# A four-layer graph network on one Trainium2 core: transfers of 127 rows in two parts, a first stage with x on ScalarE's queue, and earlier score matrices

## The chip, the core and the metric

The kernel runs on one core of a Trainium2 chip. Such a core has TensorE (PE in the profile; its weight loads are shown apart as PEld), VectorE (DVE), ScalarE (ACT), GpSimd (POOL) and SyncE (SP). Each engine runs its own instructions strictly in order and waits on semaphores for the others. SP, ACT and POOL can also issue DMA transfers, which move data between DRAM and the on-chip memories. The metric is device time in microseconds for one execution.

## The reference

The input is a node matrix x of 3327 rows and 512 columns and an adjacency matrix of 3327 x 3327 integers. Four layers are applied, each as x = x + layer(relu(layernorm(x)), adj). Layers 0, 1 and 2 are graph attention with 8, 4 and 8 heads; layer 1 adds self loops to the adjacency. Layer 3 averages over the neighbours.

```python
# one attention layer (layer 0)
Wh = jnp.einsum('nd,hdo->hno', x, W)
f1 = jnp.einsum('hno,ho->hn', Wh, a1)
f2 = jnp.einsum('hno,ho->hn', Wh, a2)
e = leaky_relu(f1[:, :, None] + f2[:, None, :], 0.2)
e = jnp.where(adj[None] > 0, e, NEG_INF)
out = elu(einsum('hnm,hmo->hno', softmax(e, axis=-1), Wh))
# the last layer
agg = (adj > 0) @ x / maximum(deg, 1)
out = relu(concat([x @ W_self + b_self, agg @ W_nb + b_nb]) @ W_comb + b_comb)
```

## The kernel before, in words

**Tiles.** The 3327 nodes are 26 tiles of 128 rows; the last tile, number 25, has 127. Target nodes are taken in chunks of four tiles (`chunks`, the last of two); source tiles come in five groups of 6, 6, 6, 4 and 4 (`JG`).

**How attention is computed.** exp(leaky_relu(s1 + s2)) is a product of a factor of the target and a factor of the source, with one pair of factors where s1 + s2 is positive and another where it isn't. So for a chunk and a head the kernel makes two 0/2 matrices in fp8 for each group: the comparison of the score row s1 with each source's score (`gt`, ACT at L656, or DVE at L653 for the source tiles in `GP_ON_DVE`), then and-ed with the adjacency mask (`tht`, L662), then the rest of the mask (L666). PE multiplies these with the source's values, which are stored as three bf16 pieces (`ab`; L694 for `tht`, L697 for `gt`).

**First stage (from L818).** For each of 26 tiles of x: load it (`first_x`, L833, on SP's queue, up to six tiles ahead, seven buffers), layernorm statistics (`norm`: DVE L318 and L322, then three small POOL steps L323 to L325 on a tile called `mv`), relu (`normed`, ACT L330), transpose on PE (L137) and copy out (`hT`, ACT L141), project with the 512 weight columns and 8 + 8 score columns (`projected`, PE L388 into PSUM tiles `acc`), scale (`scaled`) and split into pieces (`pieces`; ACT L363 and L369, DVE L359, POOL L367), and store two tiles' pieces in DRAM (L375, 1600 KB, from SP). The score columns of the weights are made at the start by `fold` in `open_layer`: products on DVE and POOL (L299) and sums on DVE (L303). In the same stage `load_mask` makes 20 adjacency blocks: load on POOL's queue (`at`, L216), transpose on PE (L221), comparison on DVE (`st`, L225), store in DRAM (`mask`, L230); `mask_tiles` then loads them as `m` (L238). Four groups of pieces for head 0 are loaded ahead in this stage (`load_pieces`, L601).

**Layers 0 to 2 (`attention`).** Loops: chunk, head, pairs of tiles of the chunk, source tiles. Between pairs `hooks.run` emits steps of other work: adjacency blocks, and the next layer's stages for tiles whose chunk is done. `open_next` loads the next layer's weights at chunk 0, head 1, behind a mark called the gate. Each head needs one broadcast score row per chunk (`s1b`, L624, 256 KB).

**Last stage.** Masks times values on PE in fp32 (L921), two DVE operations per tile (L930, L931) and the store of 512 columns (L932, SP).

**Order.** The code gives the work; a scheduler places instructions on each engine by it, by data and by the marks that `after` sets. Waits on one engine hold back all that stands behind on it, DMA issues too.

Of the kernel before, what the change touches and what calls it, by code (L numbers as in the profile page):

```python
# [52 lines left out]
def tile_gnn(ctx: ExitStack, tc: tile.TileContext, x, adj, W0, a01, W1, al, ar, W2, a2,  # L53
# [48 lines left out]
    s1d = [dram.tile([NT, H, P], F32, name=f"s1_{l}") for l, H in enumerate(heads)]  # L102
# [45 lines left out]

    stored = {}
    gone = []  # L150
# [52 lines left out]
    def load_mask(pool, t, g):  # L203


        hooks.done += 1
        n = pn(t)
        c, k = where[t]
        j0, nj = JG[g]
        w = min(nj * P, N - j0 * P)  # L210
        at = pool.tile([P, JM * P], BF16, name="at", bufs=3)
        if n < P:
            nc.vector.memset(at, 0.0)
        elif w < nj * P:
            nc.vector.memset(at[:, w:nj * P], 0.0)
        ld = nc.gpsimd.dma_start(at[:n, :w], adj[t * P:t * P + n, j0 * P:j0 * P + w])  # L216
        if gone:
            after(ld, gone[-2] if len(gone) > 1 else stored[NT - 1])
        tp = ps.tile([P, 8, P], BF16, name="tp", bufs=2)
        for j in range(nj):  # L220
            tr = nc.tensor.transpose(tp[:, j, :], at[:, j * P:(j + 1) * P], identb)  # L221
            if j == 0 and gone:
                after(tr, gone[-1])
        st = pool.tile([P, JM, P], FP8, name="st", bufs=3)
        nc.vector.tensor_scalar(st[:, :nj], tp[:, :nj], 0.0, 2.0, op0=ALU.is_gt, op1=ALU.mult, saturate=False)  # L225
        if j0 <= t < j0 + nj:
            d = pool.tile([P, P], BF16, name="d", bufs=1)
            nc.vector.tensor_tensor(d, tp[:, t - j0, :], negI, ALU.is_gt)
            nc.vector.tensor_scalar(dg1[:, t, :], d, 2.0, None, op0=ALU.mult, saturate=False)
        nc.sync.dma_start(maskd[c][g][:, k], st[:, :nj])  # L230

    def mask_tiles(c, self_loops=False, early=False):
        t0, nt = chunks[c]
        tiles, loops = [], []
        for g, (j0, nj) in enumerate(JG):
            m = mk.tile([P, PER * JM * P], FP8, name="m")
            v = m[:, :nt * nj * P].rearrange("p (k j i) -> p k j i", k=nt, j=nj)
            ld = nc.sync.dma_start(v, maskd[c][g])  # L238
            if early and c == 0:
                after(ld, stored[21])  # L240
            if self_loops:
                for k in range(nt):
                    if j0 <= t0 + k < j0 + nj:
                        loops.append((v[:, k, t0 + k - j0, :].bitcast(U32), dg1[:, t0 + k, :].bitcast(U32)))
            tiles.append(v)
# [17 lines left out]
    def open_layer(l):  # L263
# [17 lines left out]
        for i in range(2):  # L281
            av.append(pre.tile([P, 2, H2, DK], F32, name="h"))
            ld = nc.sync.dma_start(av[i].rearrange("p f h d -> p (f h) d"), a_srcs[l][i].partition_broadcast(P))
            if l:
                after(ld, stored["gate"])
        for k in range(KC):
            for f in range(2):
                dst = L.w[:, k, f, :D // 2]
                if l == 0:
                    nc.sync.dma_start(dst.rearrange("p (g o) -> p g o", g=H2),  # L290
# [6 lines left out]
        def fold(i, k):  # L297
# [3 lines left out]
            if gone:  # L301
                after(m, gone[-1])
            nc.vector.tensor_reduce(L.w[:, k, :, D // 2 + i * H2:D // 2 + (i + 1) * H2], pr, AX.X, ALU.add)  # L303
        folds = [lambda i=i, k=k: fold(i, k) for i in range(2) for k in range(KC)]
        if l:
            hooks.small = folds
        else:
            for f in folds:
                f()
# [18 lines left out]
    def normed(xt, mv, pool, behind=None):  # L328
        h = pool.tile([P, D], F32, name="h", bufs=2)
        act = nc.scalar.activation(h, xt, AF.Relu, bias=mv[:, 3:4], scale=mv[:, 2:3])  # L330
        if behind:
            after(act, behind)
        return h
# [7 lines left out]
    def pieces(L, t, AB, pool, first, behind=None):  # L341
# [32 lines left out]
        elif first and o == two - 1:  # L374
            stored[t] = nc.sync.dma_start(abd[l][g][:, :, js, :].rearrange("h p j w -> p h j w"), pt).ins.name  # L375
# [3 lines left out]
    def projected(L, t, hT, first):  # L379
# [4 lines left out]
        pws = []  # L384
        for f in range(2):
            pw = (accs if first else ps).tile([P, D // 2 + H], F32, name="acc" if first else "mm")
            for k in range(KC):
                L.mm = nc.tensor.matmul(pw, hT[:, k, :], L.w[:, k, f, :], start=(k == 0), stop=(k == KC - 1)).ins.name  # L388
# [3 lines left out]
            pws.append(pw)  # L392
# [43 lines left out]
    def project_last(L, t, hT, i, behind=None):  # L436
# [10 lines left out]
        if i == 0:  # L447
            def add():
# [4 lines left out]
                nc.sync.dma_start(y1d[c][kk * P:kk * P + n, :], y[:n])  # L453
# [10 lines left out]
    def send_s1(L, t, pool, first):  # L464
# [10 lines left out]
        (nc.sync if first else nc.gpsimd).dma_start(s1d[L.l][t0:t0 + nt].rearrange("t h p -> (t h) p"), s1t[:nt * H])  # L475

    def node_stages(L, t, get_x, pool, first=False):
# [7 lines left out]
        def statistics():  # L485
            q["mv"] = norm(q["x"], pool, behind())
# [21 lines left out]
        if first:  # L508
            return [lambda: (q.update(x=get_x()), statistics(), relu()), turn,
                    lambda: parts(L, t, scaled(L, t, projected(L, t, q["hT"], first), pool, first), pool, first), send]  # L510
# [82 lines left out]
    ahead = {}  # L593

    def load_pieces(L, pool, g, h):
# [4 lines left out]
        v = tl[:, :nj * HW].rearrange("p (j w) -> p j w", j=nj)  # L600
        return v, nc.sync.dma_start(v, abd[L.l][g][h])  # L601

    def attention(L, hooks, open_next, close):
# [4 lines left out]
        masks = mask_tiles(0, l == 1, l == 0)  # L608
        for c, (t0, nt) in enumerate(chunks):
            W = nt * P  # L610
# [3 lines left out]
            for h in range(H):  # L614
# [8 lines left out]
                s1b = rp.tile([P, WMAX], F32, name="s1b", bufs=2)  # L623
                nc.sync.dma_start(s1b[:, :W].rearrange("p (k i) -> p k i", k=nt), s1d[l][t0:t0 + nt, h, :].partition_broadcast(P))  # L624
                ab = []
                for a in range(2 if l == 1 else 1):
                    row = []
                    for g, (_, nj) in enumerate(JG):
# [6 lines left out]
                        else:  # L635
                            v, ld = ahead.pop(g) if g in ahead else load_pieces(L, mp if l else bp, g, h)
                        row.append(v)
                    ab.append(row)
                if c == 0 and h == 1:
# [745 lines left out]
```

## Time and profile before

| | us |
|---|---|
| median of 3 runs (range) | 3609.15 (3607.2 to 3612.18) |
| the profiled execution, its own time | 3609.94 |
| its span, first to last instruction | 3608.1 |
| PE busy | 3470.2 |
| DVE busy | 2648.6 |
| ACT busy | 2511.8 |
| POOL busy | 603.0 |

The median is that of unprofiled runs; the profiled execution has a time of its own, and the span leaves out what lies around its instructions. Busy time is a union over the span. Instructions that only issue a DMA aren't counted as busy, though the engine's queue stands while they run. PE's granted clock was 0.988 of full speed on average.

### The profile page before, as it was taken

The numbers are of one execution on the slowest core, as the hardware profiler recorded it, in microseconds if no ns is written. First come the engines' busy times: TensorE is split into PE (matmuls) and PEld (weight loads), VectorE is DVE, ScalarE is ACT, GpSimd is POOL, SyncE is SP. The second block draws the span as 40 slices with busy tenths as digits, with TensorE's granted clock in tenths as the row PEclk, the third lists the DMA queues.
The fourth block names the chain that finished last, engine by engine and source line by source line (L and its number), as shares of the span: only waits on it lengthen the run. The fifth ranks groups of instructions, "written<-read, shape, count | busy, mean of one in ns | idle before, by whom it ended". The sixth has DMA issues, their size and how long they took to land. (4 is left out here: it accounts for less than half of the span.)

```text
span 3608.1 us, 78551 instructions
## 1 busy us (share of the span) xinstructions
PE 3470.2 (96%) x31291; PEld 3131.4 (87%) x31291; DVE 2648.6 (73%) x5227; ACT 2511.8 (70%) x4113; POOL 603.0 (17%) x855
## 2 busy tenths in 40 slices
PE   6799999999999999999999989999999999999998
PEld 5589999999999878888888869989898989876886
DVE  7688888888887779888888868867676768672211
ACT  5587787777787788888788767767676767572111
POOL 6511221111110111233222230001010101010000
PEclk9899999999999999999999999999999999999999
DMA  7687777878866877877777876655555555576331
GB/s 213 213 239 219 212 217 215 229 207 234 237 194 206 297 264 272 286 254 277 278 257 271 311 265 205 194 176 181 175 191 182 169 176 189 169 270 253 101 104 52
DMA packets 369431, 780.69 MB, mean 216 GB/s; under 512 B 35906, under 2 KB 207333, under 8 KB 368416
## 3 DMA queue, kind: packets, MB, share of 16 engines
q1 hardware_dynamic: 341024, 713.17, 59.4%
q0 software_dynamic: 28032, 62.41, 7.3%
q8 instruction: 249, 4.08, 0.4%
q14 instruction: 126, 1.03, 0.1%
HBM read 667.96 MB, written 129.64 MB: 221 GB/s over the span
## 5 line engine op out<-in xcount | busy, mean ns | idle before, releaser
L694 PE MATMUL acc<-ab,tht 128*128 128x195 bf16 (+1 forms) x10816 | 1840.4, 248 | 15.6 <-DVE tht L662 14.3
L697 PE MATMUL acc<-ab,gt 128*128 128x195 bf16 (+1 forms) x10816 | 1839.4, 248 | 6.6 <-DVE rc L734 4.3
L656 ACT ACTIVATE gt<-s1b,ks 128x512 fp8e4<-128x512 f32 (+1 forms) x2464 | 1457.4, 677 | 316.5 <-issue 158.6
L694 PEld LDWEIGHTS <-tht 128*128 128x128 fp8e4 x10816 | 1059.1, 98 | 28.9 <-DVE tht L662 15.9
L697 PEld LDWEIGHTS <-gt 128*128 128x128 fp8e4 x10816 | 1058.9, 98 | 26.5 <-issue 20.2
L662 DVE TENSOR_TENSOR tht<-gt,m 128x768 uint32<-128x768 uint32 (+3 forms) x560 | 447.4, 799 | 141.4 <-ACT gt L656 139.5
L666 DVE TENSOR_TENSOR gt<-tht,m 128x768 uint32<-128x768 uint32 (+3 forms) x560 | 448.9, 802 | 8.7
L590 ACT CAST ts<-tht 128x1536 fp32r<-128x1536 fp8e4 x208 | 300.3, 1471 | 55.9 <-PE acc L687 51.7
L687 PE MATMUL acc<-ab,ts 128*128 128x258 f32 x2496 | 334.2, 290 | 4.4 <-ACT ts L590 2.3
L653 DVE TENSOR_SCALAR gt<-s1b,ns 128x512 fp8e4<-128x512 f32 (+1 forms) x448 | 222.2, 501 | 149.6 <-PE acc L697 147.9
L687 PEld LDWEIGHTS acc<-ab,ts 128*128 128x128 f32 x2496 | 314.1, 191 | 13.4 <-ACT ts L590 3.0
L921 PE MATMUL acc<-y,mf 128*128 128x512 f32 x1352 | 309.8, 391 | 1.6 <-DVE mf L916 1.6
L656 ACT ACTIVATE tht<-s1b,ks 128x512 fp8e4<-128x512 f32 (+1 forms) x504 | 308.5, 681 | 2.8 <-DMA s1b<-s 2.3
L921 PEld LDWEIGHTS acc<-y,mf 128*128 128x128 f32 x1352 | 253.5, 188 | 57.8 <-DVE mf L916 2.0
L712 DVE TENSOR_REDUCE R<-acc 128x130 f32<-128x390 f32 x416 | 214.5, 555 | 91.6 <-PE acc L697 91.0
L797 POOL TENSOR_TENSOR xt<-xt,e 128x512 f32<-128x512 f32 x72 | 122.2, 1697 | 888.8 <-DVE e L796 567.5
L690 PE MATMUL acc<-ab,tht 128*128 128x387 bf16 x1248 | 226.1, 329 | 6.0 <-DVE tht L662 3.2
L918 ACT CAST mf<-m 128x768 fp32r<-128x768 fp8e4 (+1 forms) x78 | 59.1, 762 | 245.1 <-PE acc L921 233.3
L687 PE MATMUL acc<-ab,tv 128*128 128x258 f32 x1664 | 220.0, 283 | 3.3 <-DMA ab<-ab 2.2
L687 PEld LDWEIGHTS acc<-ab,tv 128*128 128x128 f32 x1664 | 207.5, 189 | 6.2 <-issue 2.1
L388 PE MATMUL mm<-w,hT 128*128 128x260 f32 (+1 forms) x832 | 198.4, 393 | 9.3 <-ACT hT L141 5.6
L690 PEld LDWEIGHTS <-tht 128*128 128x128 fp8e4 x1248 | 117.3, 98 | 83.3 <-DVE tht L662 3.6
(141 smaller groups left out, 3421.4 us busy)
## 6 DMA issues: line engine op xcount, KB each, us to landing
ab<-ab SPq DMA_DIRECT2D x336, 600.0 KB, 5.6
ab<-ab SPq DMA_DIRECT2D x224, 400.0 KB, 4.1
ab<-ab SPq DMA_DIRECT2D x112, 774.0 KB, 6.3
ab<-ab SPq DMA_DIRECT2D x112, 516.0 KB, 5.5
ab<-ab SPq DMA_DIRECT2D x56, 582.0 KB, 6.6
s1b<-s SPq DMA_DIRECT2D x120, 256.0 KB, 6.2
m<-mask SPq DMA_DIRECT2D x72, 384.0 KB, 4.2
ab<-pt SPq DMA_DIRECT2D x13, 1600.0 KB, 7.6
```

What stands on the lines that cost most here:

```text
L388: L.mm = nc.tensor.matmul(pw, hT[:, k, :], L.w[:, k, f, :], start=(k == 0), stop=(k == KC - 1)).ins.name
L590: (nc.scalar.copy if KIND[g] == "s" else nc.vector.tensor_copy)(t[:, :k1 - k0, :nj], th[a][g][:, k0:k1])
L653: nc.vector.tensor_scalar(gv[:, :, jj, :], s1v, L.ns2[:, j, h:h + 1], 2.0, op0=ALU.is_gt, op1=ALU.mult, saturate=False)
L656: nc.scalar.activation(gv[:, :, jj, :], s1v, AF.Relu, bias=L.ks2[:, j, h:h + 1], scale=BIG, saturate=False)
L662: nc.vector.tensor_tensor(pu, gu, mu, ALU.bitwise_and)
L666: nc.vector.tensor_tensor(gu, pu, mu, ALU.bitwise_xor)
L687: mm = nc.tensor.matmul(acc[k][:, :2 * DA], thr[g][:, k - ks[0], jj, :], ab[a][g][:, jj, :], start=(j == 0), stop=(j == NT - 1), skip_grou ...
L690: mm = nc.tensor.matmul(acc[k][:, :3 * DA], th[a][g][:, k, jj, :], ab[a][g][:, jj, :3 * DA], start=(j == 0), stop=(j == NT - 1), skip_grou ...
L694: nc.tensor.matmul(acc[k][:, :3 * DA + o], th[0][g][:, k, jj, :], ab[0][g][:, jj, :3 * DA + o], start=(j == 0), stop=False, skip_group_che ...
L697: mm = nc.tensor.matmul(acc[k][:, AO:AO + 3 * DA + o], th[1][g][:, k, jj, :], ab[0][g][:, jj, AO:AO + 3 * DA + o], start=False, stop=(j == ...
L712: nc.vector.tensor_reduce(R[:, k], v.rearrange("p a (s d) -> p a d s", s=3), AX.X, ALU.add)
L921: nc.tensor.matmul(acc[k], mf[:, jj, :], y2[g][:, jj, s, :], start=(j0 + jj == 0 and s == 0), stop=(j0 + jj == NT - 1 and s == 1))
```

## The change

It has these parts.

- **127 rows.** A new helper `move` issues a transfer of n rows as two: the largest multiple of 16 and the rest. It is used for the load of x in the first stage, for `load_x`, for the store and the load of `y1`, for the load of `xo` and for the output. For 127 rows these are 112 and 15. `finish`, which stores from POOL, is left as it was.
- **First stage, start.** The folds are emitted after the first two stages of tiles 0 and 1. Half of the weights and one of the two score vectors are loaded from ACT's queue. Tiles 0 and 1 are projected in two steps: the 256 weight columns, and later the 8 score columns of each half.
- **First stage, x.** Tiles from 2 on are loaded from ACT's queue, each behind the relu of an earlier tile, and up to six tiles ahead.
- **First stage, masks and pieces.** The 20 blocks are taken group by group. They are written straight into the mask tiles of chunk 0, and stored in DRAM for the later layers. Head 0's pieces are copied from `pt` on the chip (13 copies) in place of being loaded back.
- **First stage, matrices.** The score row of chunk 0, head 0 is loaded in the stage, and the matrices of the first three groups are made there, one step per turn of the loop.
- **Adjacency.** `load_mask` becomes `mask_steps` with two steps, `load` and `turn`; `in_steps` puts the load of a block one hook ahead of its turn.
- **Score rows.** The DRAM tensor of s1 is laid out by chunk, head, tile, so that a broadcast row is one run of 2 KB and no longer four of 512 B.
- **Gate.** The next layer's loads stand at head 3 of chunk 0 in layers 0 and 2.

```diff
-    s1d = [dram.tile([NT, H, P], F32, name=f"s1_{l}") for l, H in enumerate(heads)]
+    s1d = [[dram.tile([H, nt, P], F32, name=f"s1_{l}_{c}") for c, (_, nt) in enumerate(chunks)]
+           for l, H in enumerate(heads)]
...
+    def move(eng, to, src, n):
+        m = n - n % 16
+        ld = eng.dma_start(to[:m], src[:m])
+        return [ld] if m == n else [ld, eng.dma_start(to[m:n], src[m:n])]
...
+    def mask_steps(pool, t, g):
...
+        q = {}
...
+        def load():
+            at = q["at"] = pool.tile([P, JM * P], BF16, name="at", bufs=3)
+            if n < P:
+                nc.vector.memset(at, 0.0)
+            elif w < nj * P:
+                nc.vector.memset(at[:, w:nj * P], 0.0)
+            ld = nc.gpsimd.dma_start(at[:n, :w], adj[t * P:t * P + n, j0 * P:j0 * P + w])
+            after(ld, gone[-1] if gone else stored[NT - 1] if c else relus[-3])
+        def turn():
+            hooks.done += 1
+            at = q["at"]
+            tp = ps.tile([P, 8, P], BF16, name="tp", bufs=2)
+            for j in range(nj):
+                tr = nc.tensor.transpose(tp[:, j, :], at[:, j * P:(j + 1) * P], identb)
+                if j == 0 and gone:
+                    after(tr, gone[-1])
+            st = masks0[g][:, k] if c == 0 else pool.tile([P, JM, P], FP8, name="st", bufs=3)[:, :nj]
...
+            nc.sync.dma_start(maskd[c][g][:, k], st)
+        return load, turn
+    def mask_view(c, g):
+        nt, nj = chunks[c][1], JG[g][1]
+        m = mk.tile([P, PER * JM * P], FP8, name="m")
+        return m[:, :nt * nj * P].rearrange("p (k j i) -> p k j i", k=nt, j=nj)
...
-            ld = nc.sync.dma_start(av[i].rearrange("p f h d -> p (f h) d"), a_srcs[l][i].partition_broadcast(P))
+            ld = (nc.sync if l or i == 0 else nc.scalar).dma_start(av[i].rearrange("p f h d -> p (f h) d"),
+                                                                   a_srcs[l][i].partition_broadcast(P))
...
-                    nc.sync.dma_start(dst.rearrange("p (g o) -> p g o", g=H2),
+                    (nc.scalar if f else nc.sync).dma_start(dst.rearrange("p (g o) -> p g o", g=H2),
                                       W0[f * H2:(f + 1) * H2, k * P:(k + 1) * P, :].rearrange("h p o -> p h o"))
...
-            if gone:
-                after(m, gone[-1])
+            if gone or i:
+                after(m, gone[-1] if gone else relus[1])
...
+        hooks.small = [lambda i=i, k=k: fold(i, k) for k in range(KC) for i in range(2)]
...
+            if g not in ahead:
+                ahead[g] = pieces_tile(L, bp, g)
+            nc.sync.dma_start(ahead[g][:, js], pt[:, 0])
             stored[t] = nc.sync.dma_start(abd[l][g][:, :, js, :].rearrange("h p j w -> p h j w"), pt).ins.name
...
+    def products(L, pws, hT, o, e):
+        for f, pw in enumerate(pws):
+            for k in range(KC):
+                mm = nc.tensor.matmul(pw[:, o:e], hT[:, k, :], L.w[:, k, f, o:e], start=(k == 0), stop=(k == KC - 1))
+                if o and k == 0:
+                    after(mm, L.mm)
+                L.mm = mm.ins.name
...
+        full = D // 2 + H
+        if pws:
+            products(L, pws, hT, D // 2, full)
+        else:
+            pws = [(accs if first else ps).tile([P, full], F32, name="acc" if first else "mm") for f in range(2)]
+            products(L, pws, hT, 0, D // 2 if first and t < 2 else full)
+            if first and t < 2:
+                return pws
...
-                nc.sync.dma_start(y1d[c][kk * P:kk * P + n, :], y[:n])
+                move(nc.sync, y1d[c][kk * P:kk * P + n, :], y, n)
...
-        (nc.sync if first else nc.gpsimd).dma_start(s1d[L.l][t0:t0 + nt].rearrange("t h p -> (t h) p"), s1t[:nt * H])
+        (nc.sync if first else nc.gpsimd).dma_start(s1d[L.l][c].rearrange("h t p -> t h p"), s1t[:nt * H])
...
-            q["mv"] = norm(q["x"], pool, behind())
+            q["mv"] = norm(q["x"], pool, relus[-2] if first and t > 1 else behind())
...
+            stages = [lambda: (q.update(x=get_x()), statistics(), relu(), get_x(7 if t else 2)), turn,
+                      lambda: parts(L, t, scaled(L, t, projected(L, t, q["hT"], first, q.get("pws")), pool, first), pool,
+                                    first), send]
+            if t == 0:
+                stages.insert(2, lambda: q.update(pws=projected(L, t, q["hT"], first)))
+            elif t == 1:
+                stages[1] = lambda: (turn(), q.update(pws=projected(L, t, q["hT"], first)))
+            return stages
...
+    def matrices(L, nt, h, g, s1v, mask, pt, gt):
...
+        def compare(jj):
+            j = j0 + jj
+            if j in GP_ON_DVE[l]:
+                nc.vector.tensor_scalar(gv[:, :, jj, :], s1v, L.ns2[:, j, h:h + 1], 2.0,
+                                        op0=ALU.is_gt, op1=ALU.mult, saturate=False)
+            else:
+                nc.scalar.activation(gv[:, :, jj, :], s1v, AF.Relu, bias=L.ks2[:, j, h:h + 1], scale=BIG,
+                                     saturate=False)
+        def split():
+            nc.vector.tensor_tensor(pu, gu, mu, ALU.bitwise_and)
+            if l != 1:
+                nc.vector.tensor_tensor(gu, pu, mu, ALU.bitwise_xor)
+        return pv, gv, (pu, mu), [lambda jj=jj: compare(jj) for jj in range(nj)] + [split]
...
+    def score_rows(l, t0, nt, h):
+        s1b = rp.tile([P, WMAX], F32, name="s1b", bufs=2)
+        v = s1b[:, :nt * P].rearrange("p (k i) -> p k i", k=nt)
+        nc.sync.dma_start(v, s1d[l][where[t0][0]][h].partition_broadcast(P))
+        return v
...
-        masks = mask_tiles(0, l == 1, l == 0)
+        masks = mask_tiles(0, l == 1) if l else masks0
...
+                s1v = early.pop("s1") if "s1" in early else score_rows(l, t0, nt, h)
...
-                if c == 0 and h == 1:
+                if c == 0 and h == (1 if l == 1 else 3):
                     stored["gate"] = ld.ins.name
                     N_ = open_next()
...
+                for g in range(len(JG)):
+                    if g in early:
+                        pv, gv = early.pop(g)
...
+        for ld in move(nc.gpsimd if behind else nc.sync, xt, x_rows(l, t), n):
+            if behind or l == 0:
+                after(ld, behind or gone[0])
...
+    def in_steps(work):
+        return [lambda ss=[work[i - s][s] for s in (1, 0) if 0 <= i - s < len(work)]: [s() for s in ss]
+                for i in range(len(work) + 1)]
...
-                nc.sync.dma_start(xt[:pn(u)], x_rows(0, u))
+                for ld in move(nc.scalar if u > 1 else nc.sync, xt, x_rows(0, u), pn(u)):
+                    if relus:
+                        after(ld, relus[-1])
...
-        hooks.masks = [lambda t=t, g=g: load_mask(ip, t, g) for t in range(NT) for g in range(len(JG))]
-        hooks.tiles = [node_stages(L, t, lambda t=t: first_x(t), fp, True) for t in range(NT)]
-        n = 0
+        masks0 = [mask_view(0, g) for g in range(len(JG))]
+        order = [(t, g) for g in range(len(JG)) for t in range(PER)]
+        order += [(t, g) for t in range(PER, NT) for g in range(len(JG))]
+        hooks.masks = in_steps([mask_steps(ip, t, g) for t, g in order[:20]])
+        hooks.tiles = [node_stages(L, t, lambda lead=1, t=t: first_x(t, lead), fp, True) for t in range(NT)]
+        folds, hooks.small = hooks.small, []
+        for n in range(2):
+            hooks.run(1, 0, 0)
+        for f in folds:
+            f()
         while hooks.tiles or hooks.flying:
-            hooks.run(1, 0, 1 if n >= 4 and hooks.done < 20 else 0)
-            for g, (j0, nj) in enumerate(JG[:-1]):
-                if n == j0 + nj + 2:
-                    ahead[g] = load_pieces(L, bp, g, 0)
             n += 1
+            hooks.run(1, 0, 1 if n >= 4 else 0)
+            if n == 7:
+                early["s1"] = score_rows(0, 0, PER, 0)
+            for g in range(3):
+                if n == (8, 15, 21)[g]:
+                    if g == 0:
+                        b = pre.tile([P, KC, 2 * WW], F32, name="w").rearrange("p c o -> p (c o)")
+                    else:
+                        b = pre.tile([P, 8, 1, 400], BF16, name="pt", bufs=2).rearrange("p h o w -> p (h o w)")
+                    b = b.bitcast(FP8)
+                    s = PER * JM * P
+                    pv, gv, _, steps = matrices(L, PER, 0, g, early["s1"], masks0[g], b[:, :s], b[:, s:2 * s])
+                    hooks.small += steps
+                    early[g] = pv, gv
+        while hooks.small:
+            hooks.small.pop(0)()
...
-                    nc.sync.dma_start(out[t * P:t * P + n, :], o[:n])
+                    move(nc.sync, out[t * P:t * P + n, :], o, n)
```

`hooks.small` takes one step per call of `hooks.run`, so the first-stage matrices are made one comparison at a time. `matrices` holds what stood in the body of `attention` before.

## The prediction

> **What bounds the kernel now.** I read the page first: busy shares and the chain that ended last.
>
> ```profile
> span 3608.1 us, 78551 instructions
> PE 3470.2 (96%) x31291; PEld 3131.4 (87%) x31291; DVE 2648.6 (73%) x5227; ACT 2511.8 (70%) x4113; POOL 603.0 (17%) x855
> PE acc L921 8%; DVE o L930 0%; DVE o L931 0%; DVE mf L916 0%
> ```
>
> TensorE (PE) is the bound: it idles 137.9 us of 3608.1. An edit that shortens other engines' work is worth only what it takes out of that idle. The chain names the last stage alone, so I next asked for the stretches of the span (length; busy time per engine; granted clock; DMA share; GB/s), to see where PE idles.
>
> ```profile
> 0.00:16.25 16.25, 0.00 (x0) 0.00 (x0) 7.36 (x18) 2.14 (x3) 8.08 (x22) 1.00 0.87 231
> ...
> 29.40:124.00 94.60, 78.32 (x413) 64.14 (x411) 66.26 (x139) 61.30 (x133) 64.77 (x110) 0.95 0.77 222
> 124.00:142.00 18.00, 6.58 (x19) 5.04 (x17) 6.87 (x14) 4.75 (x10) 6.11 (x10) 0.62 0.39 126
> ...
> 176.50:189.20 12.70, 3.62 (x23) 3.00 (x23) 9.38 (x16) 10.84 (x20) 5.27 (x7) 0.60 0.80 246
> 189.20:3293.60 3104.40, 3039.54 (x29336) 2779.40 (x29334) 2462.23 (x4870) 2347.68 (x3812) 491.41 (x661) 0.99 0.71 228
> ...
> 3593.20:3608.10 14.90, 0.00 (x0) 0.00 (x0) 0.02 (x1) 0.00 (x0) 0.00 (x0) 0.58 0.06 20
> ```
>
> First PE number of each row against its length: the first 189.2 us lose 56.6 us, the last 14.9 us are lost whole, and the 3104 us between lose only 64.9 us. The first stage and the tail are where time is to be had. The waits of the first 190 us and the PE timeline say who holds PE (start, length, work, [idle before]):
>
> ```profile
> DVE st L318 <- DMA xt<-in_x_dram: 26.3, 11, 10.7
> PE tp L137 <- ACT h L330: 16.3, 1, 16.3
> ACT h L330 <- POOL mv L325: 15.3, 3, 10.7
> ```
>
> ```profile
> 135.56 6.72 PE L388 MATMUL acc<-w,hT 128*128 128x264 f32 x16 [11.42 <-ACT hT L141]
> ...
> 172.14 3.83 PE L388 MATMUL acc<-w,hT 128*128 128x264 f32 x16 [1.06 <-ACT hT L141]
> ...
> 185.07 0.83 PE L694 MATMUL acc<-ab,tht 128*128 128x196 bf16 x4 [8.56 <-DVE tht L662]
> ```
>
> The 11.42 us comes after VectorE (DVE) waited 10.7 us for the last x tile, the 127-row one (issued 117.8, used 131.8). While it moves, and from 3596 to 3606 after the last store (also 127 rows), the DMA share is 0.07 at 25 GB/s: one engine of 16. After each pause the projection takes 6.72 instead of 3.83 us at a lower clock.
>
> **The Trainium skill.** "DMA: Bandwidth & Descriptors", section on why a DMA increments its semaphore by 16: a copy from SP or ScalarE (ACT) runs on the largest number up to 16 that divides the slowest dimension of both patterns, so 127 rows use 1 engine, 112 use 16 and 15 use 15; POOL's copies are excepted. The trace agrees: share 0.07 above, and POOL's 254 KB load took 4.9 us. Same page, "Issuing engines are not separate DMA queues": another queue saves only issue time; bandwidth is not what I count on. "TensorE: Matmul & The Clock Gate", section on the clock gate: after idling, PE runs at half clock until it has been busy for about 3.4 us; the 0.60 clock of 176.5 to 189.2 agrees.
>
> **The change part by part** (against the profiled execution, 3609.9 us for its span of 3608.1).
>
> *Tail.* The last store is issued at 3593.2 and lands 12.7 us later, the longest of its line; the median of the other 256 KB stores is 2.7 us. In two parts: one more issue (0.3 us), then 2.7 us. Gain 12.7 - 3.0 = 9.7 us. The 127-row loads and store of y1 and x in the last stages show no wait on PE: 0.
>
> *Start.* Now PE begins at 16.25 because POOL does weight products (L299) and adjacency issues before the three small mv steps. The change puts mv of tiles 0 and 1 first and the products behind. Statistics end at 5.1; two each of 0.23, 0.57, 0.26 us on POOL give about 7.2; relu 0.8: PE transposes at 8. Half of W goes out on ACT, so 2 MB (x, a, W) at the 250 GB/s seen land at about 10. Two tiles of 3.83 us plus about 3 us at low clock end near 20. Then comes what the change adds: the 8 score columns are multiplied apart, 16 matmuls in the program, 32 in the trace, each not below its 0.19 us weight load: 6.1 us. The folds (4 x 1.28 us on POOL, 12 x 0.68 on DVE) finish at about 17, before these. So 26, and with transposes tile 2's product starts at 26.5 instead of 31.48. Gain 5, from 2 to 8.
>
> *Tiles 2 to 25.* Product of tile 2 (31.48) to the end of tile 25 (175.97) is 144.5 us for 24 tiles. Of it 11.4 + 2.9 us are the 127-row load and its slow restart; the stalls at 60 and 97 (3.3 and 3.7 us, with 1.7 and 2.5 us of slow clock) follow DVE waits of 4.2 and 2.6 us for xt, whose loads stood on SP behind stores that wait for POOL. On ACT's queue, issued after the relu and about six tiles ahead (some 25 us against 4.5 us to landing), all 25.5 us go; 119 us, or 4.96 a tile, remain. What the change adds: ACT was busy 3.81 of 4.90 us in the clean tile from 143.4. It gets one x issue a tile (296 to 1654 ns, median 425 on SP; none seen on ACT, bounds 0.05 and 1.65 us; I take 0.7, as many are 1.0 to 1.2 just after a big store) and 16 score comparisons (34.40 us / 56 = 0.61 us each, 0.41 a tile). 3.81 + 0.7 + 0.41 = 4.92: no slack. Queued behind a waiting x issue are the hT copies, for which PE waits. DVE gets three pairs of mask operations (1.92 us each) and 2 comparisons, 6.8 us over the stage, hidden by its 0.9 us a tile of slack. So I take 5.45 us a tile instead of 4.96: 24 x 5.45 = 131, end at 157.3. POOL's adjacency issues are as many as before; SP's stage loads of masks (5) go, and 13 piece copies replace 5 loads of pieces: near equal bytes, hidden by a DMA share of 0.77.
>
> *Attention's start.* Before, 9.1 us from 175.97 to 185.07, then 0.5 us, and about 2.0 us at half clock: as if it began at 187.6. Now three groups of matrices are made within the stage, enough for 18 x 4 matmuls at 83 ns, 6 us, while ACT makes group 3 (3 x 0.61) and 4. The accumulators come free with DVE's reading of tile 24. I allow 1.5 us: 158.8. From start, tiles and this together: 187.6 - 158.8 = 28.8 us. If the cover fails, the old 9 us come back.
>
> *Adjacency a hook ahead.* One wait at 683.58 is [4.21 <-DMA at], with about 1.8 us of slow clock (0.91 over 20 us) behind it. A load one hook (about 8 us) earlier, against 7.3 us from issue to use, covers it: 5. Later ones show 0.4 us.
>
> *Later head, 2 KB runs, a second POOL issue per layer (0.6 us).* PE loses 0.8 us near 200 to 215, where head 1's loads are, and nothing to s1b; SP's issues move to head 3, where PE is 99% busy. The eight folds of the next weights still fit into the ten hook calls after head 3. 0, within 2 either way.
>
> Sum: 9.7 + 28.8 + 5 = 43.5. 3609.9 - 43.5 = 3566.4; the shown median, 3609.15, lies 0.8 below the profiled time: **3566**.
>
> **Rivals.** (a) ACT becomes the bound of the first stage: at 6.3 us a tile the end is 177.7, 20.4 us later, giving 3586. For: 4.92 us of work in a strict order. Against: the 0.7 is SP's figure with its queue behind big stores. (b) The split does not spread: the tail's 9.7 us stay, 3576; tile 25's load stays hidden by its lead. Against: the skill's rule. (c) Attention still waits at its start (masks or pieces late): 9 us, 3575. (d) Slower: the x issues wait on ACT for the landing of SP's 1.6 MB stores (7.1 us median), which then hold hT. It decides from the point where the stage eats all other gains: 43.5 + 7.2 = 50.7 us over 24 tiles, 2.1 us more, 7.6 us a tile, giving 3616. Against: a slot is used again only some 2.5 tiles, 12 us, later.
>
> **How the numbers follow.** About 0.2% (7 us) is what a measurement can tell from no change. Chances: forecast 0.64, own range 3554 (4.96 a tile, start 1.5 us earlier) to 3573 (5.7 a tile); (a) 0.17; (b) 0.06; (c) 0.07; (d) 0.04; several losses that cancel the gain 0.02. The range takes in (b), (c) and most of (a): 3552 to 3586. Faster 0.94, same 0.02, slower 0.04.
>
> **What would show it.** PE's first transpose near 8 and tile 2's product near 26.5; no DVE wait above 1 us for xt; ACT above 90% from tile 2 on; the last projection near 157, attention within 2 us of it at full clock; no wait for at near 680; the end some 5 us after the last DVE operation. A stage end after 170, or ACT waiting on its DMA issues, would make it wrong.

## The result, and the profile after

The changed kernel took 3608.77 us (median of 20 runs, 3600.35 to 3620.72), the kernel before 3609.06 us (median of 20, 3602.73 to 3614.02). The ratio is 0.9999, 95% interval 0.9991 to 1.0007: no difference, where 3566 was forecast. Its profiled execution took 3606.74 us, its span is 3.1 us shorter than that of the kernel before.

The page of the changed kernel: the span, the engines' busy time, and the lines of the chain that ended last.

```profile
span 3605.0 us, 78609 instructions
PE 3480.3 (97%) x31323; PEld 3143.9 (87%) x31323; DVE 2660.0 (74%) x5227; ACT 2512.7 (70%) x4113; POOL 633.4 (18%) x858
PE acc L751 9%; PE acc L748 9%; PE acc L1002 8%; PE mm L471 4%; ACT gt L652 1%; DVE tht L656 1%; DVE gt L658 1%; DVE R L766 0%; DMA y<-AB 0%; POOL xt L851 0%; DVE gt L649 0%; PE tp L138 0%; DVE e L850 0%; PE mm L190 0%; ACT e L848 0%
```

The same stretches of its span (length; busy time and count of PE, PEld, DVE, ACT, POOL; granted clock; DMA share; GB/s), the last one ending with the span:

```profile
0.00:16.25 16.25, 7.18 (x27) 6.11 (x28) 8.91 (x20) 3.98 (x5) 5.15 (x20) 1.00 0.82 225
...
29.40:124.00 94.60, 78.23 (x410) 64.44 (x410) 81.69 (x151) 70.53 (x150) 72.01 (x110) 0.95 0.84 242
124.00:142.00 18.00, 14.94 (x67) 11.76 (x66) 15.83 (x28) 12.16 (x27) 14.98 (x22) 0.84 0.63 174
...
176.50:189.20 12.70, 8.67 (x96) 7.46 (x93) 7.80 (x21) 12.70 (x22) 2.38 (x5) 0.94 1.05 309
189.20:3293.60 3104.40, 3026.93 (x29124) 2768.84 (x29124) 2449.29 (x4840) 2329.15 (x3778) 512.91 (x665) 0.99 0.69 227
...
3593.20:3605.00 11.80, 3.72 (x17) 2.75 (x15) 1.44 (x2) 0.00 (x0) 0.00 (x0) 0.83 0.09 28
```

The stretches that the prediction aimed at did get better: PE is busy 152.4 of the first 189.2 us instead of 132.6, and the stretch with the 127-row load went from 6.58 to 14.94. But the long middle, 189 to 3294, is busy 12.6 us less than before. What PE waits for (total us, times, longest) says where:

```profile
PE tp L234 <- DMA at<-in_adj_dram: 30.6, 11, 5.1
PE acc L398 <- ACT hT L142: 12.8, 13, 3.9
PE tp L138 <- ACT h L342: 11.4, 3, 9.1
```

The first line was 4.6 us in 2 waits before. It is the adjacency tile whose load was to come earlier. The timeline around one such wait, and the attention's start (start, length, engine, work, [idle before]):

```profile
164.90 0.25 PE L748 MATMUL acc<-ab,w 128*128 128x196 bf16 x1
...
737.83 0.50 PE L234 MATMUL tp<-identb,at 128*128 128x128 bf16 x6
740.12 1.60 POOL L226 DMA_DIRECT2D at<-in_adj_dram  x3
744.83 0.82 PE L234 MATMUL tp<-identb,at 128*128 128x128 bf16 x6 [5.07 <-DMA at<-in_adj_dram]
```

The same block (the 97th) in the kernel before, its load and its transposes:

```profile
726.38 0.62 POOL L216 DMA_DIRECT2D at<-in_adj_dram  x1 [0.19 <-issue]
744.96 0.50 PE L221 MATMUL tp<-identb,at 128*128 128x128 bf16 x6
```

Before, the load went out 18.6 us ahead of its transposes. After, PE ran dry at 739.76 (744.83 less 5.07), POOL issued at 740.12, 4.7 us ahead, and PE stood for the landing. (Loads and transposes are paired by their order.) Of the 110 blocks behind the first stage, one had a lead under 6 us before and nine have it after; the median hardly moved, 17.2 and 16.8 us. The lead became shorter for a few blocks, and at the median no longer.

Segments read off both traces, by the first or last product of each layer, against the forecast (minus is a gain). As in the prediction, the attention of the kernel before counts as begun at 187.6.

| segment | before, us | after, us | difference | forecast |
|---|---|---|---|---|
| to the attention's start | 187.6 | 164.9 | -22.7 | -28.8 |
| layer 0's attention | 1071.1 | 1103.5 | +32.4 | -5 |
| change to layer 1 | 19.3 | 19.4 | +0.1 | 0 |
| layer 1's attention | 841.4 | 837.4 | -4.0 | 0 |
| change to layer 2 | 24.2 | 20.9 | -3.3 | 0 |
| layer 2's attention | 1109.5 | 1110.3 | +0.8 | 0 |
| last stage and tail | 355.0 | 348.6 | -6.4 | -9.7 |
| sum | 3608.1 | 3605.0 | -3.1 | -43.5 |

Layer 1's attention takes 837 to 846 us in all the runs below, whatever the edit, so its 4.0 us are not read further. So the question for the experiments is what layer 0's attention gave back, and why the first stage fell 6 us short.

### The profile page after: what moved, and what is told of

Read it like the earlier page. It is cut to its first block, busy times and chain, and to the rows that moved or that the text cites. A ratio compares the mean times of both kernels' runs of the same rounds, so it can differ in the third digit from the quotient of the medians.

```text
span 3605.0 us, 78609 instructions
## 1 busy us (share of the span) xinstructions
PE 3480.3 (97%) x31323; PEld 3143.9 (87%) x31323; DVE 2660.0 (74%) x5227; ACT 2512.7 (70%) x4113; POOL 633.4 (18%) x858
## 5 line engine op out<-in xcount | busy, mean ns | idle before, releaser
L751 PEld LDWEIGHTS <-gt 128*128 128x128 fp8e4 x10744 | 1055.4, 98 | 28.6 <-issue 19.4
L748 PEld LDWEIGHTS <-tht 128*128 128x128 fp8e4 x10744 | 1055.4, 98 | 19.8 <-DVE tht L656 7.3
L380 POOL TENSOR_TENSOR pt<-r 128x520 bf16<-128x520 f32 (+1 forms) x116 | 136.6, 1198 | 318.0 <-DVE r L372 301.1
```

The source lines that it names most:

```text
L748: nc.tensor.matmul(acc[k][:, :3 * DA + o], th[0][g][:, k, jj, :], ab[0][g][:, jj, :3 * DA + o], start=(j == 0), stop=False, skip_group_che ...
L751: mm = nc.tensor.matmul(acc[k][:, AO:AO + 3 * DA + o], th[1][g][:, k, jj, :], ab[0][g][:, jj, AO:AO + 3 * DA + o], start=False, stop=(j == ...
```

## The experiments

Each comparison is with the kernel before on the same chip. The chips differ a little (its median was 3609.4, 3606.8, 3612.5 and 3608.1 us in the four groups below), so ratios are compared, and segments of the traces.

### The adjacency loads: e1, e2, e3

The theory is that the edit works against itself. A block is the adjacency of one target tile and one group of source tiles. A pass is one head's products for a pair of target tiles; `gone` lists the last product of each pass. A hook is the call of `hooks.run` behind a pass. `in_steps` moves the load one *block* ahead. The mark of the load (the point on another engine's order behind which the scheduler puts it) went from `gone[-2]` to `gone[-1]`, one pass later. Where a hook runs one block, the two cancel. Where it runs two (every second hook in chunk 0, every third later), load and transposes of a tile then stand in the same gap between two passes. e1 puts the old mark back:

```diff
-            after(ld, gone[-1] if gone else stored[NT - 1] if c else relus[-3])
+            after(ld, gone[-2] if len(gone) > 1 else stored[NT - 1] if c else relus[-3])
```

> The changed kernel with one word different: an adjacency load in the attention is held behind the pass before the last one (gone[-2]), as in the kernel before, and not behind the last pass (gone[-1]). Theory 1 (the block moved the load one block earlier but the new mark moved it one pass later, so that load and transposes stand in the same gap between two passes and TensorE sits out the landing): TensorE's waits for the adjacency tile fall from 30.6 us to under 8, and the time from 3608.8 to about 3584 (3576 to 3590). Rival A (the loads are slow to land because the queues of layer 0's attention are fuller after the change): the waits stay over 20 us and the time over 3602. Rival B (the waits are only where a loss shows that another engine would take over, as at the layer boundaries): the waits fall, but DVE's or ACT's take their place and the time stays over 3600.

e2 leaves the mark, and puts the transposes two blocks behind their load in the attention:

```diff
-    hooks.masks = in_steps([mask_steps(ip, t, g) for t, g in order[20:]])
+    late = [mask_steps(ip, t, g) for t, g in order[20:]]
+    hooks.masks = [lambda ss=[late[i - d][s] for s, d in ((1, 2), (0, 0)) if 0 <= i - d < len(late)]: [s() for s in ss]
+                   for i in range(len(late) + 2)]
```

> The changed kernel with the mark left as it is (gone[-1]) and the transposes two blocks behind their load instead of one, so that no load has its own transposes in the same gap even where a hook runs two blocks. Theory 1: the load leads by at least one hook (about 8 us against 5 to 6 us to land), the waits for the adjacency tile fall from 30.6 us to under 8 and the time to about 3583 (3575 to 3590), like the run with the earlier mark. Rival A (slow landings): at 8 us of lead still over 15 us of waits, 3595 or more. Rival C (the mark itself, not the lead, costs: GpSimd's queue is held at the mark and other work behind it is late): no gain, about 3609.

e3 is the other direction, the kernel before with this part alone:

```diff
-    hooks.masks = [lambda t=t, g=g: load_mask(ip, t, g) for t in range(NT) for g in range(len(JG))][hooks.done:]
+    late = [mask_steps(ip, t, g) for t in range(NT) for g in range(len(JG))][hooks.done:]
+    hooks.masks = [lambda ss=[late[i - s][s] for s in (1, 0) if 0 <= i - s < len(late)]: [s() for s in ss]
+                   for i in range(len(late) + 1)]
```

with `load` marked `gone[-1]` as in the change.

> The kernel before with only the adjacency part of the change in the attention: load and transposes are two steps, a block holds the transposes of one load and the issue of the next, and the load is marked behind the last pass. Theory 1: this part alone makes the waits for the adjacency tile grow from 4.6 to about 30 us and costs 26: about 3635 (3625 to 3642). Rival A (the waits come from what the new first stage and the two-part transfers put on the queues): waits under 10 us and 3603 to 3612; the gain of 5 that the prediction gave this part would show as about 3604.

| | median, us | ratio to before (95%) | layer 0's attention, us |
|---|---|---|---|
| changed kernel | 3608.77 | 0.9999 (0.9991 to 1.0007) | 1103.5 |
| e1, old mark | 3576.53 | 0.9911 (0.9897 to 0.9926) | 1069.4 |
| e2, two blocks behind | 3574.17 | 0.9898 (0.9885 to 0.9911) | 1069.2 |
| e3, before plus this part | 3631.71 | 1.0062 (1.0050 to 1.0074) | 1095.6 (before, also from its first product: 1073.6) |

PE's waits for the adjacency tile, first in the page of e3, then within e1's attention of layer 0:

```profile
PE tp L225 <- DMA at<-in_adj_dram: 26.9, 10, 4.4
```

```profile
PE tp L234 <- DMA at<-in_adj_dram: 1.2, 1, 1.2
```

In e2's timeline the lead is there, 18.8 us from the first of these two issues to its transposes, and no wait:

```profile
695.75 1.05 POOL L226 DMA_DIRECT2D at<-in_adj_dram  x2 [6.08 <-issue]
...
714.53 0.39 PE L234 MATMUL tp<-identb,at 128*128 128x128 bf16 x4
```

Leads under 6 us: one block of the 110 in e1 and in e2, eight in e3. All three went as the theory said, e2 to just below its range: taking the short lead away gains 32 and 35 us (by the medians), adding it costs 22. Rivals A and B would have left e1 above 3600, rival C e2 at 3609. The price is more than the waits. From 189.2 us to the end of layer 0's attention the changed kernel takes 1079.2 us and e2 1049.5: 20.0 us of the 29.7 are PE idle (39.6 against 19.6), and 9.7 us are longer busy time (1039.6 against 1029.9, mean clock 0.98 against 0.99) for about the same count of products, which fits slow restarts after the waits.

### The first stage's queue: e6, c2, c3, d1

e6 is the changed kernel with the first stage's loads on SyncE's queue:

```diff
-                for ld in move(nc.scalar if u > 1 else nc.sync, xt, x_rows(0, u), pn(u)):
+                for ld in move(nc.sync, xt, x_rows(0, u), pn(u)):
```

and the same for `a_srcs[l][1]` and half of W.

> The changed kernel with all loads of the first stage on SyncE's queue as before (x tiles from the third, the second score vector, half of the weights), nothing else moved. The prediction put the tile rate at 5.45 us and measured is 5.68. If the issues on ScalarE's own queue cost the stage its 0.2 us a tile (24 tiles, 5 us) then the time falls to about 3604; if they bring the 3 us of the earlier start and no loss, it grows to about 3612; if the queue does not matter, 3608 to 3610.

It took 3596.99 us, 0.9965 (0.9953 to 0.9978): a gain of 12, more than any of the three cases said. Layer 0's attention stayed at 1106.5 us, and PE's waits for the adjacency tile at 31.8 us. The gain is all in the first stage: the attention starts at 152.06 instead of 164.90.

c2 joins e2 and e6; c3 is c2 with the loads of the weights and the second score vector back on ScalarE, so that only the x tiles are moved.

> The changed kernel with the transposes two blocks behind their load (as in e2) and all first-stage loads on SyncE's queue (as in e6). Theory (two independent losses, one in layer 0's attention and one in the first stage): the gains add, 3608.8 - 34.6 - 11.8 = 3562 (3557 to 3567). Rival (the second one overlaps the first, as less time before the attention means less cover later): only 3 to 6 us below e2's 3574, 3568 to 3572.

> As the run before, but only the x tiles go back to SyncE's queue; half of the weights and the second score vector still start on ScalarE's. Theory 1 (the x issues among ScalarE's work are the loss: tile rate 5.68 against 5.25 us, 24 tiles, about 10 us): like the run before, 3562 to 3565. Rival (the start is the loss: the product of tile 2 begins at 28.5 us with ScalarE's loads and at 26.2 with SyncE's, and what follows is late for it): about 3571 to 3574, little gained on e2.

c2: 3562.33 us, 0.9872 (0.9852 to 0.9891). c3: 3561.60 us, 0.9867 (0.9849 to 0.9886). The two losses are independent and add, and it is the x tiles alone. c3 beats both kernels by 1.3%. From the first product of tile 2 to the attention's start, in the changed kernel and then in c3 (columns as in the stretches):

```profile
28.53:164.90 136.37, 114.97 (x583) 94.42 (x583) 115.01 (x209) 99.45 (x212) 99.02 (x149) 0.94 0.77 226
```

```profile
30.49:156.59 126.10, 109.06 (x584) 90.27 (x584) 110.70 (x209) 98.79 (x212) 99.97 (x146) 0.99 0.81 240
```

24 tiles at 5.68 and at 5.25 us. Single traces of this stretch vary: with x on ScalarE's queue it took 136.4 to 141.5 us (the changed kernel, e1, e2), with x on SyncE's 125.9 to 130.3 (e6, c2, c3, d3, h1, h2). The two kinds lie further apart than the runs of one kind. ScalarE's busy time is the same (99.45 and 98.79), so what differs is how long it stands. d1 asks whether the issue's time or its waits do it. It adds to c3 an idle copy on ScalarE (extra work that no other kernel has) where each x issue stood:

```diff
+                if u > 1:
+                    cp = nc.scalar.copy(spare, ident.unsqueeze(1).to_broadcast([P, 2, P]))
+                    if relus:
+                        after(cp, relus[-1])
```

> The fastest kernel so far (c3, 3561.6: transposes two blocks behind the load, x tiles on SyncE's queue) with an idle copy of 128 x 256 (estimated at 0.35 us from the 0.56 us of a 128 x 512 copy) put on ScalarE at each place where the change issues an x tile there: it takes ScalarE's time as the 0.34 us issue did, but waits for nothing. Theory 1 (ScalarE's time itself is the loss, as it is the bound of the tile loop): 24 times 0.35 and the order it brings, 8 to 12 us, 3570 to 3574. Rival (what the issues wait for is the loss: they stand on ScalarE until a buffer or an earlier transfer is free, and the copies for TensorE stand behind them): 3561 to 3565.

d1: 3568.11 us, 0.9875 (0.9858 to 0.9891), against c3's 0.9867: 3 us of difference, within both intervals, and between the two cases that were expected. The same stretch in d1:

```profile
29.59:158.06 128.47, 109.22 (x583) 90.36 (x583) 112.19 (x209) 102.83 (x228) 99.21 (x146) 0.99 0.79 236
```

16 of the 24 copies lie in it (ScalarE's count is 228 instead of 212), 0.39 us each, 6.3 us together, and it is 2.4 us longer; h2, without the copies, took 128.4 as well, so even this is not clear of the spread. In the changed kernel 16 x issues of 0.33 us and one more part lie in its stretch, 6 us together, and it is 10.3 us longer than c3's. So time on ScalarE is the smaller part; what the issues wait for, and the order that they bring, is the larger. In the trace of the changed kernel 22 of the 25 x issues on ScalarE wait for one of eight semaphores that tell of the landing of SyncE's loads and stores too, so an x issue can stand until a store of SyncE has landed. ScalarE's timeline in e2 shows such a case:

```profile
92.48 1.15 ACT L376 COPY pt<-AB 128x520 bf16<-128x520 bf16 x2
96.31 0.34 ACTq L153 DMA_DIRECT2D xt<-in_x_dram  x1
96.69 1.16 ACT L382 COPY pt<-r 128x520 bf16<-128x520 bf16 x2 [3.06 <-DMA ab<-pt]
```

ScalarE stands from 93.63 to 96.31, until a piece store has landed, with the x issue first in its order. The copy behind it may have needed the same landing, so this case is an indication and no proof; waits and order were not measured apart.

### The split: e5, e4

e5 is the kernel before with `move` (112 + 15 rows) in its 127-row transfers; e4 the changed kernel with `m = n` in `move`, so that all go in one part.

```diff
-        m = n - n % 16
+        m = n
```

> The kernel before with the two-part transfers alone. The prediction's terms: 9.7 us at the tail and 14.3 us at tile 25's load in the first stage (11.4 of wait and 2.9 of slow restart), so about 3585 (3582 to 3590). Rival b (the split does not spread over the DMA engines): 3606 to 3612. Rival c (only the tail gains, since tile 25's load starts late and not only runs long): 3598 to 3601.

> The changed kernel with all transfers in one part again. If the split is worth its tail alone there (8.1 instead of 16.4 us from the last matmul to the end) and tile 25's load is hidden by its lead: 3617 (3615 to 3620). If the lead does not hide tile 25's load, it is worth the 11 to 14 us of the kernel before as well: 3626 to 3632. If it does not spread: 3609.

e5: 3589.57 us, 0.9943 (0.9928 to 0.9958). Its attention starts at 168.47 instead of 185.07, and from the last DVE operation to the end it takes 6.6 instead of 14.9 us. Both terms are there, 8.3 at the tail and 16.6 at the stage, where 9.7 and 14.3 were said. e4: 3624.50 us, 1.0040 (1.0026 to 1.0054), 15 us above the changed kernel by the ratios. That lies between its first two cases. Its tail is 8.1 us longer. Its attention starts at 172.47, 7.6 us later than in the changed kernel and 3 to 5 us later than in e1 and e2, whose first stage has the same code; of the 16.6 us in e5 the lead of six tiles hides half or more. Rival b falls in both.

### Matrices made early, later head, longer rows: d2, d3, d4, h1, h2

All five start from c3. d2 leaves the three groups of matrices to the attention's start. d3 undoes the later head and the 2 KB rows together, h1 the head alone, h2 the rows alone. d4 puts the transposes two blocks behind in the first stage too.

```diff
# d2
-                if n == (8, 15, 21)[g]:
+                if n < 0:
# d3 and h1
-                if c == 0 and h == (1 if l == 1 else 3):
+                if c == 0 and h == 1:
# d3 and h2, with the store and the load of the rows to match
-    s1d = [[dram.tile([H, nt, P], F32, name=f"s1_{l}_{c}") for c, (_, nt) in enumerate(chunks)]
+    s1d = [[dram.tile([nt, H, P], F32, name=f"s1_{l}_{c}") for c, (_, nt) in enumerate(chunks)]
```

> The same fastest kernel, but the three groups of the first head's matrices are not made within the first stage; they are made at the attention's start as in the kernel before (masks still kept in place). The prediction gave the start of the attention 9.1 + 2.5 - 1.5 us of gain and charged 0.41 us a tile of ScalarE's time for it. Theory: the wait comes back (8 to 9 us with a slow restart of 2) and the stage gets 16 ScalarE operations of 0.61 us shorter, which give 0 to 10 us back: net 0 to 9 us slower, 3562 to 3571. Rival (the matrices in the stage cost as much as they save): same as c3, 3559 to 3564.

> The same fastest kernel, with two parts undone together: the next layer's loads start at head 1 again in all layers, and the score rows lie in 512-byte runs. The prediction put both at 0, within 2: 3560 to 3564. If the later head or the longer runs were worth what they take from the DMA engines near 200 to 215 us, it is 3566 or more; if the later head costs at a layer's end, 3558 or less.

> The same fastest kernel, with the transposes two blocks behind their load in the first stage too (TensorE waits 3.6 us there behind mask compares of VectorE, 3 times). If these come from the adjacency tile landing late: 3558 to 3560; if they come from VectorE's own order: no change, 3560 to 3564.

> The fastest kernel (c3, span 3564.1) with the next layer's loads at head 1 again, score rows left in 2 KB runs. d3, with both undone, lost 5 us of TensorE waits in the first 60 us of the attention and layer 0 took 1075.9 instead of 1069.0 us. Theory (the head: its ten loads on SyncE's queue stand ahead of the third head's score rows there): layer 0 takes 1074 to 1077 us again, the time is about 3572 (3567 to 3579). Rival (the rows): layer 0 takes 1068 to 1070 us and the time is 3559 to 3565.

> The fastest kernel (c3) with the score rows in 512-byte runs again, the later head left in. Theory (the head is what d3 lost): layer 0 takes 1068 to 1070 us, 3559 to 3566. Rival (the rows): layer 0 takes 1074 us or more, 3568 or more. If both share it, each gives 1071 to 1073.

| | median, us | ratio to before (95%) | attention starts | layer 0's attention, us | change to layer 2, us |
|---|---|---|---|---|---|
| c3 | 3561.60 | 0.9867 (0.9849 to 0.9886) | 156.59 | 1069.0 | 20.5 |
| d2 | 3569.80 | 0.9882 (0.9866 to 0.9899) | 163.93 | 1066.5 | 21.0 |
| d3 | 3578.90 | 0.9910 (0.9894 to 0.9927) | 159.50 | 1075.9 | 22.9 |
| d4 | 3569.04 | 0.9876 (0.9860 to 0.9893) | 162.72 | 1067.3 | 20.7 |
| h1 | 3567.90 | 0.9890 (0.9873 to 0.9906) | 155.24 | 1074.5 | 20.6 |
| h2 | 3569.86 | 0.9899 (0.9883 to 0.9916) | 156.63 | 1066.1 | 24.2 |

d2: the wait at the attention's start comes back, and the stage's tiles get only about 0.07 us shorter. Its timeline there:

```profile
163.93 0.83 PE L748 MATMUL acc<-ab,tht 128*128 128x196 bf16 x4 [9.31 <-DVE tht L656]
```

The start is 7.3 us later, 5 us of it left by the end of layer 0. By the ratios the loss, 5 us, is inside both intervals; the trace carries it.

d3, h1 and h2: what was put at nothing is worth something. By the ratios d3 is 15 us slower than c3, the intervals apart; h1 is 8 and h2 12 us slower, their intervals overlapping c3's. The traces show the two parts in different places. The head: with the next layer's loads at head 1, layer 0's attention takes 5.5 us more in h1 and 6.9 in d3; in all eight runs with a real lead and the later head it takes 1066 to 1071 us. SyncE's timeline of d3 and then of c3 shows the score rows of the third head behind these loads, or ahead of them:

```profile
175.82 9.50 SPq L311 DMA_DIRECT2D w<-in_L_gnn_W_dram  x8
185.37 0.43 SPq L170 DMA_DIRECT2D w<-in_L_gnn_W_comb_dram  x1
185.91 0.44 SPq L664 DMA_DIRECT2D s1b<-s  x1
```

```profile
171.74 0.39 SPq L664 DMA_DIRECT2D s1b<-s  x1
```

In h1 PE then waits near the start for what c3 does not (c3 has 0.8 us for the first):

```profile
PE tp L234 <- DMA at<-in_adj_dram: 2.8, 1, 2.8
PE acc L751 <- DVE gt L658: 2.4, 2, 1.5
```

The rows: h2's time fell in its rival's range, but not where the rival had the loss. Layer 0's attention is 2.9 us shorter (1066.1), and the change to layer 2 takes 24.2 instead of 20.5 us, as long as in the kernel before. PE's timeline there in h2, then in c3:

```profile
2106.70 1.12 PE L138 MATMUL tp<-ident,h 128*128 128x128 f32 x4 [3.23 <-ACT h L342]
2110.76 0.84 PE L748 MATMUL acc<-ab,tht 128*128 128x195 bf16 x4 [2.94 <-DVE tht L656]
```

```profile
2108.25 0.51 PE L748 MATMUL acc<-ab,tht 128*128 128x195 bf16 x4 [3.08 <-DVE tht L656]
```

In h2 a tile's transposes stand ahead of the layer's first products and wait 3.23 us for their input; in c3 they come behind. That is a matter of where the scheduler put them, not of a transfer that got faster. d4 gained nothing and fell in neither of its cases: its tiles took 5.6 us instead of 5.25 and the attention started 6.1 us later; why was not looked into. These differences of a few us are read from one trace each.

## Why the prediction was wrong

**The step that failed** is *Adjacency a hook ahead*: "A load one hook (about 8 us) earlier, against 7.3 us from issue to use, covers it: 5." I took the name of the edit for its effect. The load moved one block ahead and its mark one pass later. Where a hook runs one block, that is no gain; where it runs two, one of the blocks lost its lead, 4.7 us instead of 18.6 in the case shown, which was too short for the landing. The diff showed both lines; I priced one. The 7.3 us that I took as the lead was also an exception: the median lead was 17.2 us already. And the wait at 683.58, which it was to remove, came back in the changed kernel one block earlier, 4.29 us at 679.11. In place of a gain of 5 the runs show a loss of 32 to 35 us (e1, e2), 22 on the kernel before (e3). This term turns the forecast round: without the loss the changed kernel is e1 or e2, faster by 32 to 35 us. Even for a lead that works no run shows the 5: h1, with the lead and the next layer's loads at head 1 as before, took 1074.5 us for layer 0's attention, the kernel before 1073.6 from its first product; what e1 and e2 gain on that, 4 us, is no more than the later head brings. No rival named the loss. My slower rival was in the first stage, and I held the middle, PE 97.9% busy, for a place where little could happen. e3 shows what such a place costs: PE waited 22.3 us more for the adjacency tile than in the kernel before, and the layer took 22.0 us longer.

**Tiles 2 to 25**, 5.45 us a tile: 5.68 measured, near the edge of its own range, but for another reason. ScalarE was to be above 90% busy and the bound. It was busy 99.45 of 136.37 us, 73%, and 77% with its x issues, which took 0.33 us and not 0.7. Rival (d)'s mechanism, x issues that stand on ScalarE for the landing of SyncE's stores, fits what d1 and e2 show; I set it aside because a slot would be free long before, though I had named such waits as a sign of being wrong. Its size was less than the 50.7 us which that rival needed: 0.43 us a tile, about 10 us, and 12 in the runs of e6. My claim that ScalarE's queue was needed to remove the stalls at 60 and 97 us (11.2 us with their slow clock) was also wrong. In c3 the x tiles are on SyncE's queue, the tiles take 5.25 us, and PE's longest wait in the loop is 2.4 us. The split alone (e5, x on SyncE's queue) brought the 24 tiles from 144.5 to 127.7 us, 16.8 of the 25.5 that I had counted, without another queue. Which edit takes the rest was not tried.

**Start**: PE's first transpose at 9.07 instead of 8, tile 2's product at 28.53 instead of 26.5; the gain was 3 of the 5, inside its range. c3, with half of W on ScalarE, has 30.49, and c2, without, 28.20: no gain from the second queue is seen. **Attention's start**: right in kind. The attention began at full clock as the stage ended, at 164.90, and d2 shows the wait of 9.31 us that the early matrices remove. Start, tiles and this gave 22.7 of the 28.8 us.

**Tail**: right, 8.3 us instead of 9.7. The mechanism agrees with the Trainium skill ("DMA: Bandwidth & Descriptors", section on why a DMA increments its semaphore by 16), by which a tile of 127 partitions runs on one DMA engine and one of 128 on 16: with the last 127-row store in parts of 112 and 15 rows, the end comes 6.6 instead of 14.9 us after the last DVE operation (e5). e5 and e4 agree at both places where it counts. The page excepts some of the copies that GpSimd issues, not all of them as the prediction has it; nothing here rests on that.

**Later head, 2 KB runs**: 0, within 2, was mis-sized. The head is worth 5.5 us in layer 0. The rows are worth 3.7 us at the change to layer 2, by the order that they bring there; the 2.9 us that h2 is ahead in layer 0 go against them, so the net is open.

Put together from the runs: -35 us for a real lead, -12 for x on SyncE's queue. What was left of the change would have been 3562, near the 3566 forecast, so the balance was lost in two places, one of which I had not priced as a loss at all. That forecast and rest lie so close is luck in part, as the term of 5 and the 0 for the head were both off.

## What to carry to other kernels

When a step is moved ahead, work out its lead in both orders that decide it, the order in which the program emits it and the mark it is held behind, and count from issue to use in the busiest case (here the hooks that run two blocks). A gain in a stage with slack can be given back in full where the bounding engine is 98% busy: here eleven late transfers did it. Before a load goes on the queue of an engine that computes, ask what its issue will wait for: the engine's own work stands behind it.

## What was not expected of the hardware

The same x loads were issued and landed faster on ScalarE's queue, and the kernel was slower for it: 0.33 us an issue and 3.2 us to landing (medians in the tile loop, changed kernel) against 1.19 and 7.1 us on SyncE's (e6). The traces show the landing of only 5 and 4 of these loads. The Trainium skill ("DMA: Bandwidth & Descriptors", "Issuing engines are not separate DMA queues") says that another issuing engine only saves the time it takes to initiate the DMA; here 0.9 us an issue was saved, and 12 us of the run were lost on an engine whose order the tiles depend on. And 6.3 us of idle copies on ScalarE, already busy for 78% of the tile loop, lengthened it by 2.4 us, within the spread of such traces.
